# Cross-attention block in fp32: bias copies placed ahead of the normalised rows, and three early steps placed anew

## The chip, the cores and the metric

The kernel runs on one core of a Trainium2 chip. The metric is device time in microseconds (us) of one execution; lower is better. Before the change the median of three runs is 1100.1 us (1099.98 to 1101.31).

A core has five engines that run side by side: TensorE (PE; its weight loads are shown apart as PEld), VectorE (DVE), ScalarE (ACT), GpSimd (POOL) and SyncE (SP). Here SyncE issues every transfer (DMA). Each engine works through its own instructions in the order of the program and waits on semaphores where it needs another's result.

## The reference

Sixteen batches, each of 1024 query rows and 64 context rows, width 512, 16 heads of width 32. Query rows and context rows are each normalised, scaled and shifted by a conditioning vector; then cross-attention, a projection and a residual:

```
xq  = (1 + scale_q)  * layernorm(x)       + bias_q      # scale, bias from silu(cond) @ Wss_q
xkv = (1 + scale_kv) * layernorm(context) + bias_kv
q = xq @ Wq + bq ;  k, v = xkv @ Wkv + bkv
out = x + (softmax(q k^T / sqrt(32)) v) @ Wp + bp
```

All is fp32; x is (16, 1024, 512).

## The kernel before

**Tiles and stages.** The 16384 query rows are cut into 32 blocks of 512 (`NB = 32`; two blocks a batch, four tiles of 128 rows a block). Keys and values are made for two batches at a time, since 2 x 64 context rows fill the 128 partitions. A block i passes through these steps, each a small function in the code:

- `load_x` (L127) fetches its rows; `q_stats` (L260, VectorE) takes mean and variance; `q_scale` makes the factors (ScalarE, VectorE, GpSimd); `hidden` (L281, ScalarE) writes the normalised rows, two tiles a call.
- `turn` (L409, VectorE) and `move` (L421, SyncE) transpose them: 32x32 transposes into the one `ht` buffer, then 16 transfers of 64 KB into `xt`.
- `queries(i, o)` (L452): four matmuls of 128x512 into a PSUM bank, copied out to `qt` by ScalarE (L479). `query_weights` folds the scale into Wq first.
- `scores(i, z)` (L483): 32 small matmuls for one half of the keys; VectorE takes maxima (L501), then ScalarE copies the scores to SBUF (L508).
- `maxima`, `subtract` (spread on VectorE, L522, then GpSimd, L535), `weights` (L541, the exponential on ScalarE), `sums` (L546, VectorE), `inverse` and `divide` (L566, GpSimd).
- `mix(i)` (L570): 64 small matmuls, weights times values, copied out to `ot` by ScalarE.
- the projection. Blocks 0 and 1, and the last ones, use `project` (L610), four matmuls of 128x512 for each row tile. The loop, for blocks 2 to 28, uses seven products of half-size blocks instead of eight (`product`, L696), with three sums of half rows on VectorE (`row_sums`, L680), one on GpSimd (`last_row_sum`), and sums of the halves of Wp made once by `weight_sums` (L638, four subtractions on GpSimd into `WT`, and `b_diff`).

**Order of work.** It is written out by hand, under a manual schedule: the functions are called in the order in which each engine is to issue. A prologue handles blocks 0 to 2, a loop handles i = 3 to 29, and an end part the last two. In a turn i of the loop, the scores of block i, the queries of block i+1, mix and products of block i-1 and normalisation of block i+2 are interleaved.

**The projection's bias.** For i > 3 the loop calls `biased(i - 1)` (L661): two ScalarE copies (L665), which put the second half of the bias and the difference of its halves into PSUM banks 2 and 3; products 1 and 2 then accumulate onto them. In turn 3 there is no such call; products 1 and 2 start their banks themselves, and GpSimd adds the bias to the residual rows (`residual`, L286). Later blocks get the rest by one GpSimd add (`residual_rest`, L655). `added` (L724, VectorE) adds a bank to the residual rows. Query banks come from banks 0 and 1 in the loop (`ring`).

**The queue.** SyncE issues all transfers in program order. Eight completion semaphores are used in turn, so a transfer is issued only when the one eight places before it has landed. The Wp load (`load_projection`, L176) stands between the bias load and `move(1)`.

The calls in the loop around which the change is made:

```python
        hidden(i + 2, (0, 1))      # L897
        mix(i - 1)
        mixed_halves(i - 1)        # L677, L678
        hidden(i + 2, (2, 3))
        if i > 3:
            biased(i - 1)          # L902
        ...
        queries(i + 1, 1)          # L914
        product(i - 1, 1, first=i == 3)
        product(i - 1, 2, first=i == 3)
```

Of the kernel before, what the change touches and what calls it, by code (L numbers as in the profile page):

```python
# [20 lines left out]
def cross_attention_block(  # L21
# [101 lines left out]
    def rows_of(a, i):  # L123
        b, s = divmod(i, BPB)
        return a[b, s * TB : (s + 1) * TB, :].rearrange("(t p) h -> p t h", p=P)

    def load_x(i):  # L127
        t = xpool.tile([P, NT, H], F32, tag="x", name=f"x_{i}")
        nc.sync.dma_start(t, rows_of(x, i))
        x_tiles[i] = t  # L130

    def load_residual(i):

        tag = "r" if i < NB - 1 else "x"
        r = xpool.tile([P, NT, H], F32, tag=tag, name=f"r_{i}")
        nc.sync.dma_start(r, rows_of(x, i))
        r_tiles[i] = r
# [38 lines left out]
    def load_projection():  # L176
        nc.sync.dma_start(w_p_sb, w_p.rearrange("(c p) o -> p c o", p=P))
# [66 lines left out]
    def row_stats(mv, r):  # L244
        bs = small.tile([P, 6], F32, tag="bs", name="bs")
        nc.vector.bn_stats(bs, r)  # L246
        nc.vector.bn_aggr(mv, bs)

    def rstd_of(mv, n, tag):

        rstd = small.tile([P, 2, n], F32, tag=f"rstd{tag}", name=f"rstd{tag}")
        nc.scalar.activation(rstd[:, 0, :], mv[:, :, 1], AF.Sqrt, bias=eps_sb)
        nc.vector.reciprocal(rstd[:, 0, :], rstd[:, 0, :])
        nc.gpsimd.tensor_tensor(rstd[:, 1, :], mv[:, :, 0], rstd[:, 0, :], ALU.mult)
        nc.gpsimd.tensor_scalar(rstd[:, 1, :], rstd[:, 1, :], -1.0, None, ALU.mult)  # L255
        return rstd
# [3 lines left out]
    def q_stats(i, ts=range(NT)):  # L260
        if ts[0] == 0:
            q_mv[i] = small.tile([P, NT, 2], F32, tag="mvq", name=f"mvq_{i}")
        for t in ts:
            row_stats(q_mv[i][:, t, :], x_tiles[i][:, t, :])

    def q_scale(i):
        q_rstd[i] = rstd_of(q_mv.pop(i), NT, "q")
# [13 lines left out]
    def hidden(i, ts):  # L281

        for t in ts:
            normalise(x_tiles[i][:, t, :], x_tiles[i][:, t, :], q_rstd[i], t)

    def residual(i, ts=range(NT)):  # L286
        for t in ts:
            nc.gpsimd.tensor_add(r_tiles[i][:, t, :], r_tiles[i][:, t, :], b_p_sb)
# [9 lines left out]
    def context_features(b):  # L298
        hk = hk_tiles.pop(b)
        pt = bank(f"pkt_{b}")  # L300
        for c in range(NC):
            nc.tensor.transpose(pt[:, c * P : (c + 1) * P], hk[:, c * P : (c + 1) * P], ident)
        xk = kvpool.tile([P, NC, P], F32, tag="xk", name=f"xk_{b}")
        sk = ss["kv"]
        for c in range(NC):
            for j in range(2):
                at = c * P + j * LKV
                nc.scalar.activation(
                    xk[:, c, j * LKV : (j + 1) * LKV],
                    pt[:, at : at + LKV],  # L310
                    AF.Identity,
                    scale=sk[:, c, b + j : b + j + 1],
                    bias=sk[:, NC + c, b + j : b + j + 1],
                )
        xk_tiles[b] = xk
# [105 lines left out]
    def move(i):  # L421

        ht = ht_tiles.pop(i)
        xt = qpool.tile([P, 4, NC, NT * 32], F32, tag="xt", name=f"xt_{i}")
        for k in range(4):
            for g in range(4):
                nc.sync.dma_start(  # L427
                    xt[32 * k : 32 * k + 32, g],
                    ht[32 * g : 32 * g + 32, k].rearrange("p c t b -> p c (t b)"),
                )  # L430
        xt_tiles[i] = xt
# [20 lines left out]
    def queries(i, o, spare=False, later=False):  # L452

        xt, b = xt_tiles[i], i // BPB
        if o == 0:
            qt_tiles[i] = qpool.tile([P, NC, TB], F32, tag="qt", name=f"qt_{i}")
        if spare:
            pq = ps_s.tile([P, 2, TB], F32, tag="s", name=f"pq_{i}_{o}")[:, 0, :]
        else:
            pq = bank(f"pq_{i}_{o}")  # L460
        for c in range(NC):
            nc.tensor.matmul(  # L462
                pq.rearrange("p (g n) -> p g n", g=4),
                lhsT=wq_tiles[b][:, c, o * P : (o + 1) * P],
                rhs=xt[:, :, c, :],
                start=(c == 0),
                stop=(c == NC - 1),
            )
        pq_tiles[i, o] = pq
        if not later:  # L470
            queried(i, o)
# [61 lines left out]
    def subtract(i, eng=nc.gpsimd, zs=(0, 1)):  # L533
        for z in zs:
            eng.tensor_tensor(s_tiles[i, z], s_tiles[i, z], mb_tiles[i], ALU.subtract)  # L535
# [3 lines left out]
    def weights(i, z):  # L539
        p = s_tiles[i, z]  # L540
        nc.scalar.activation(p, p, AF.Exp, scale=SCALE)  # L541
# [96 lines left out]
    def weight_sums():  # L638
        t1, t2, t3, t4 = (WT[:, j] for j in range(4))
        nc.gpsimd.tensor_tensor(t1, half_weights(0, 1), half_weights(0, 0), ALU.subtract)  # L640
        nc.gpsimd.tensor_tensor(t2, half_weights(1, 1), t1, ALU.subtract)
        nc.gpsimd.tensor_tensor(t3, half_weights(1, 1), half_weights(0, 1), ALU.subtract)
        nc.gpsimd.tensor_tensor(t4, half_weights(1, 0), t2, ALU.subtract)
        nc.gpsimd.tensor_tensor(b_diff, b_first, b_second, ALU.subtract)
# [16 lines left out]
    def biased(i):  # L661

        for k, n, b in ((2, 1, b_second), (3, 2, b_diff)):
            acc[k] = bank(f"pp_{i}_{n}", k)
            nc.scalar.copy(acc[k].rearrange("p (t h) -> p t h", t=2), twice(b))  # L665
# [96 lines left out]
    load_x(2)  # L762
    load_residual(0)
    load_projection_bias()
    load_projection()
    for h in range(2):
        scale_shift_rows("kv", h)
    turn(1, range(NT))
    move(1)
    load_x(3)  # L770
    queries(0, 2)
    for h in range(2):
# [13 lines left out]
    load_x(4)  # L786
    load_residual(1)
    residual(0)
    weight_sums()
    value_products(0)  # L790
    scores(0, 1)
    maxima(0)
# [50 lines left out]
    scores(2, 1)  # L843
    maxima(2)
    subtract(2)
    hidden(4, (2, 3))
    project(0, 3)
    queries(3, 0)
# [5 lines left out]
    mix(1)  # L854
    mixed(1)
    q_stats(5)
    queries(3, 3)
    weights(2, 0)
    project(1, 0)
    sums(2, 0)  # L860
    weights(2, 1)
    residual(2, (0, 1))
    project(1, 1)
    sums(2, 1)
    inverse(2)
    divide(2)
    q_scale(5)
    context_features(2)
    query_weights(2)
    project(1, 2)  # L870
# [2 lines left out]
    for i in range(3, NB - 2):  # L873
        nxt3 = i + 3 < NB
        kvb = i // 4 * 2 + 2
        kv = i % 4 if kvb < B else None
        if nxt3:
            load_x(i + 3)
        if kv == 0:
            load_context(kvb)  # L880
        if i > 3:
            added(i - 2, 5)
        scores(i, 0)
        if i > 3:
            product(i - 2, 4)
            added(i - 2, 4)
            product(i - 2, 3)
            added(i - 2, 3)
        else:
            project(i - 2, 3)  # L890
            ring[:] = [0, 1]
        scores(i, 1)
        maxima(i)
        subtract(i)
        queries(i + 1, 0)
        load_residual(i)
        hidden(i + 2, (0, 1))  # L897
        mix(i - 1)
        mixed_halves(i - 1)
        hidden(i + 2, (2, 3))  # L900
        if i > 3:
            biased(i - 1)  # L902
        if kv == 1:
            context_hidden(kvb)
        if nxt3:
            q_stats(i + 3)
        if kv == 0:
            kv_stats(kvb)
        row_sums(i - 1)
        turn(i + 2, range(NT))  # L910
        move(i + 2)
        if not nxt3:
            load_residual(NB - 1)
# [3 lines that stand above are left out]
        weights(i, 0)  # L917
        added(i - 1, 1)
        added(i - 1, 2)
        sums(i, 0)  # L920
        weights(i, 1)
        queries(i + 1, 2)
        last_row_sum(i - 1)
        if i == 3:
            residual(2, (2, 3))
        if i < NB - 3:
            residual_rest(i)
        else:
            residual(i)
        product(i - 1, 6)  # L930
        product(i - 1, 7)
        sums(i, 1)
        added(i - 1, 6)
        inverse(i)
        added(i - 1, 7)
        divide(i)
        if nxt3:
            q_scale(i + 3)
        if kv == 0:
            kv_scale(kvb)  # L940
        if kv == 2:
            context_features(kvb)
        if kv == 3:
            keys(kvb)
        queries(i + 1, 3)
        if (i + 2) % BPB == 0 and i + 2 < NB:
            query_weights((i + 2) // BPB)
        if kv == 3:
            value_products(kvb)
            value_tiles(kvb)  # L950
        product(i - 1, 5)
# [95 lines left out]
```

## Time and profile before

| what | value |
|---|---|
| median of three runs | 1100.1 us |
| the profiled execution's own time | 1099.69 us |
| its span, first to last instruction | 1097.9 us |
| TensorE busy | 1079.0 us (98%) |
| VectorE busy | 874.1 us (80%) |
| ScalarE, GpSimd busy | 656.7, 661.0 us (60% each) |
| bias copies (L665), one | 587 to 590 ns, 52 of them |
| DMA moved | 145.36 MB |

The profile comes from one execution. Times in its rows count from the start of the span. In a row of the groups or the timeline, the name before the arrow is written and those behind it are read; "x16" counts instructions. "Idle before" is the time that the engine stood still ahead of the row, with what ended it; a chain lists the work that ended last, followed back from the end. A weight load (PEld) may run under the matmul before it, and then costs nothing.

### The profile page before, as it was taken

What the parts mean: (1) busy time and instruction counts of PE and PEld (TensorE: products, weight loads), DVE (VectorE), ACT (ScalarE), POOL (GpSimd) and SP (SyncE); (2) the same over time, 40 slices, a digit from 0 to 9 for tenths busy, and PEclk for the clock granted to TensorE, in tenths of its full rate; (3) what the DMA queues carried; (4) which work ended last, traced back from release to release, by engine and by line L of the source; (5) the groups of instructions that cost most, each with busy time, mean ns of one, the idle gap of its engine ahead of it and who ended that gap; (6) DMA issues with size and microseconds to landing.
All of it is one profiled execution on the core that took longest, in us unless ns stands there. A gap on an engine that the chain in (4) does not pass through costs nothing.

```text
span 1097.9 us, 20355 instructions
## 1 busy us (share of the span) xinstructions
PE 1079.0 (98%) x8290; PEld 612.1 (56%) x8290; DVE 874.1 (80%) x1132; ACT 656.7 (60%) x804; POOL 661.0 (60%) x288
## 2 busy tenths in 40 slices
PE   6999999999999999999999999999999999999998
PEld 4534365555655557555565556555665556655533
DVE  4699678888698886989868889688887888697893
ACT  3576656657467573766736676465765657467430
POOL 0447685666747765666737666566765666748830
PEclk9999999999999999999999999999999999999999
DMA  9633432444234443344443343343342444333302
GB/s 354 218 113 116 152 122 98 143 151 153 89 110 144 141 144 112 115 135 140 137 143 125 116 142 123 130 154 119 129 144 92 144 154 136 96 109 104 134 29 87
DMA packets 80524, 145.36 MB, mean 132 GB/s; under 512 B 10504, under 2 KB 10656, under 8 KB 80432
## 3 DMA queue, kind: packets, MB, share of 16 engines
q1 hardware_dynamic: 80432, 144.07, 39.3%
q8 instruction: 65, 1.06, 0.4%
q14 instruction: 27, 0.22, 0.1%
HBM read 77.97 MB, written 33.55 MB: 102 GB/s over the span
## 4 chain that ended last, share of the span: by engine, by line
PE 92%; DMA 3%; DVE 2%; ACT 1%; SPq 1%; issue 0%; DVEq 0%
PE pq L462 38%; PE pp L715 31%; PE po L586 7%; PE ps L490 6%; PE pp L613 6%; PE pv L350 2%; PE pk L322 2%; DMA w_kv_sb<-in_L_xcond_Wkv_dram 1%; DMA w_p_sb<-in_L_xcond_Wp_dram 1%; DVE m L501 1%; SPq L144 1%; DMA x<-in_x_dram 1%; SPq L427 1%; DVE vb L522 0%; DVE l L546 0%; ACT s L541 0%
## 5 line engine op out<-in xcount | busy, mean ns | idle before, releaser
L462 PE MATMUL pq<-xt,wq 128*128 128x512 f32 x1024 | 465.9, 599 | 1.8 <-DMA xt<-ht 1.7
L566 POOL TENSOR_TENSOR s<-s,vb 128x2048 f32<-128x2048 f32 x62 | 279.9, 4536 | 192.8 <-DVE vb L522 183.4
L535 POOL TENSOR_TENSOR s<-s,mb 128x2048 f32<-128x2048 f32 x58 | 262.6, 4553 | 160.9 <-DVE mb L522 158.8
L462 PEld LDWEIGHTS pq<-xt,wq 128*128 128x128 f32 x1024 | 188.4, 190 | 244.0 <-issue 240.4
L508 ACT COPY s<-ps 128x1024 f32<-128x1024 f32 x128 | 129.6, 1012 | 196.2 <-DVE m L501 188.7
L729 DVE TENSOR_TENSOR r<-pp,r 128x512 f32<-128x512 f32 x189 | 126.4, 669 | 72.4 <-PE pp L715 71.5
L479 ACT ACTIVATE qt<-pq,bqs 128x512 f32<-128x512 f32 x128 | 87.7, 686 | 154.2 <-PE pq L462 153.4
L501 DVE TRANSPOSE_TENSOR_REDUCE m<-ps 128x32 f32<-128x1024 f32 x128 | 152.2, 1227 | 24.3 <-PE ps L490 24.3
L715 PE MATMUL pp<-w_p_sb,ot 128*128 128x256 f32 x648 | 151.4, 384 | 0.0
L546 DVE TRANSPOSE_TENSOR_REDUCE l<-s 128x64 f32<-128x2048 f32 x64 | 146.2, 2299 | 5.7 <-ACT s L541 5.2
L715 PEld LDWEIGHTS pp<-w_p_sb,ot 128*128 128x128 f32 x648 | 121.2, 190 | 35.5 <-ACT pp L665 19.9
L541 ACT ACTIVATE s<-s 128x2048 f32<-128x2048 f32 x64 | 121.9, 1910 | 21.0 <-POOL s L535 16.3
L715 PE MATMUL pp<-WT,ot 128*128 128x256 f32 x432 | 104.9, 386 | 0.0
L715 PE MATMUL pp<-WT,s 128*128 128x256 f32 x432 | 102.8, 381 | 0.0
L715 PEld LDWEIGHTS pp<-WT,s 128*128 128x128 f32 x432 | 81.6, 190 | 32.1 <-issue 19.8
L277 ACT ACTIVATE x<-x,rstdq 128x512 f32<-128x512 f32 x128 | 96.9, 810 | 1.9 <-POOL rstdq L255 1.9
L715 PEld LDWEIGHTS pp<-WT,ot 128*128 128x128 f32 x432 | 80.0, 190 | 32.3 <-DVE r L729 16.8
L246 DVE BATCH_NORM_STATS2 bs<-x 128x6 f32<-128x512 f32 x128 | 84.4, 659 | 2.2 <-DMA x<-in_x_dram 2.2
L414 DVE STREAM_TRANSPOSE ht<-x 128x512 f32<-128x512 f32 x124 | 77.5, 679 | 5.9 <-DMA xt<-ht 3.8
L522 DVE STREAM_TRANSPOSE mb<-m 128x2048 f32<-128x2048 f32 x32 | 74.0, 2312 | 6.1 <-POOL s L566 2.7
L490 PE MATMUL ps<-qt,kt 32*32 32x512 f32 x2048 | 76.6, 600 | 1.8 <-DVE kt L330 0.8
L586 PE MATMUL po<-s,vt 32*32 32x512 f32 x2048 | 76.1, 599 | 1.2 <-ACT qt L479 1.2
(94 smaller groups left out, 904.5 us busy)
## 6 DMA issues: line engine op xcount, KB each, us to landing
x<-in_x_dram SPq DMA_DIRECT2D x32, 1024.0 KB, 5.7
r<-in_x_dram SPq DMA_DIRECT2D x32, 1024.0 KB, 5.4
xt<-ht SPq DMA_DIRECT2D x496, 64.0 KB, 2.0
out_dram<-r SPq DMA_DIRECT2D x54, 512.0 KB, 2.8
out_dram<-r SPq DMA_DIRECT2D x20, 256.0 KB, 2.0
wss_q<-in_L_xcond_Wss_q_dram SPq DMA_DIRECT2D x2, 1024.0 KB, 9.0
ctx<-in_ctx_dram SPq DMA_DIRECT2D x8, 256.0 KB, 5.6
wss_kv<-in_L_xcond_Wss_kv_dram SPq DMA_DIRECT2D x2, 1024.0 KB
```

The source lines that it names most:

```text
L277: nc.scalar.activation(dst, src, AF.Identity, bias=rstd[:, 1, j : j + 1], scale=rstd[:, 0, j : j + 1])
L462: nc.tensor.matmul(pq.rearrange("p (g n) -> p g n", g=4), lhsT=wq_tiles[b][:, c, o * P : (o + 1) * P], rhs=xt[:, :, c, :], start=(c == 0), ...
L490: nc.tensor.matmul(pss[r // 2][32 * c : 32 * c + 32, r % 2, :], lhsT=kt[rows, c, z * HK : (z + 1) * HK], rhs=qt[rows, c, :], start=True, s ...
L501: nc.vector.tensor_reduce(m_tiles[i][:, z, 2 * e : 2 * e + 2, :], pss[e].rearrange("p r (j a) -> p r j a", a=32), AX.X, ALU.max, apply_tra ...
L508: nc.scalar.copy(s_sb[:, 2 * e : 2 * e + 2, :], pss[e])
L535: eng.tensor_tensor(s_tiles[i, z], s_tiles[i, z], mb_tiles[i], ALU.subtract)
L541: nc.scalar.activation(p, p, AF.Exp, scale=SCALE)
L546: nc.vector.tensor_reduce(l_tiles[i][:, z], s_tiles[i, z].rearrange("p r (j a) -> p r j a", a=32), AX.X, ALU.add, apply_transpose=True,)
L566: eng.tensor_tensor(s_tiles[i, z], s_tiles[i, z], vb, ALU.mult)
L586: nc.tensor.matmul(po[c][32 * r : 32 * r + 32, :], lhsT=vt[rows, z, 32 * r : 32 * r + 32], rhs=p[rows, r, :], start=(z == 0), stop=(z == 1),)
L715: nc.tensor.matmul(acc[k][:, t * HO : (t + 1) * HO], lhsT=rows[:, c, t * P : (t + 1) * P], rhs=cols[:, c, :], start=new and t == 0 and c == 0,
L729: nc.vector.tensor_add(r, acc[k].rearrange("p (t h) -> p t h", t=2), r)
```

## The change

Five calls of the hand-written order are placed elsewhere. No operation is added, removed or altered.

1. In the loop, `biased(i - 1)` is called ahead of `hidden(i + 2, (0, 1))`, `mix` and `mixed_halves`, no longer behind the second `hidden`.
2. `load_projection()`, the 1 MB load of Wp, is called behind `move(1)` and ahead of `load_x(3)`.
3. `weight_sums()`, which reads Wp, goes from behind `residual(0)` to behind `subtract(2)`.
4. `weights(2, 0)`, an exponential of block 2, is called ahead of `queries(3, 3)`. On TensorE this changes nothing; on ScalarE the exponential now stands before the copy of that query bank.
5. `residual(2, (0, 1))`, GpSimd's bias add for half of block 2, goes behind `divide(2)` and `q_scale(5)`.

```diff
@@ prologue
     load_projection_bias()
-    load_projection()
     for h in range(2):
         scale_shift_rows("kv", h)
     turn(1, range(NT))
     move(1)
+    load_projection()
     load_x(3)
@@
     residual(0)
-    weight_sums()
     value_products(0)
@@
     scores(2, 1)
     maxima(2)
     subtract(2)
+    weight_sums()
     hidden(4, (2, 3))
@@
     q_stats(5)
+    weights(2, 0)
     queries(3, 3)
-    weights(2, 0)
     project(1, 0)
     sums(2, 0)
     weights(2, 1)
-    residual(2, (0, 1))
     project(1, 1)
     sums(2, 1)
     inverse(2)
     divide(2)
     q_scale(5)
+    residual(2, (0, 1))
     context_features(2)
@@ loop
         load_residual(i)
+        if i > 3:
+            biased(i - 1)
         hidden(i + 2, (0, 1))
         mix(i - 1)
         mixed_halves(i - 1)
         hidden(i + 2, (2, 3))
-        if i > 3:
-            biased(i - 1)
         if kv == 1:
             context_hidden(kvb)
```

## The prediction, made before the changed kernel ran

> **What bounds the kernel now.** I read the page first: busy shares, then the chain that ended last.
>
> ```profile
> span 1097.9 us, 20355 instructions
> ...
> PE 1079.0 (98%) x8290; PEld 612.1 (56%) x8290; DVE 874.1 (80%) x1132; ACT 656.7 (60%) x804; POOL 661.0 (60%) x288
> ...
> PE 92%; DMA 3%; DVE 2%; ACT 1%; SPq 1%; issue 0%; DVEq 0%
> ```
>
> TensorE is busy nearly throughout and carries 92% of the chain. So time can come only from TensorE's few waits (early) and from matmul groups that run slower than they need. The list of all waits names both.
>
> ```profile
> PEld pp L715 <- ACT pp L665: 19.9, 26, 0.8
> ...
> DVE ht L414 <- DMA xt<-ht: 3.8, 1, 3.8
> ...
> PE pq L462 <- DMA xt<-ht: 1.7, 1, 1.7
> ```
>
> Columns: total us, times, longest. The first row is the bias copy holding the weight loader, 26 times for 0.77 us. Only part of this is lost, because the loader works under running matmuls. What is lost is seen in the chain in order of time (start, us), where turn 3 of the loop makes the same products without bias copies (145.47) and turn 4 with them (183.71):
>
> ```profile
> 141.84 3.63 PE pq L462 x8
> 145.47 3.45 PE pp L715 x16
> ...
> 180.08 3.63 PE pq L462 x8
> 183.71 3.66 PE pp L715 x16
> 187.37 3.43 PE pq L462 x8
> 190.80 3.45 PE pp L715 x16
> ```
>
> The group costs 3.66 with the copies and 3.45 without. The timeline of that place shows why:
>
> ```profile
> 181.10 0.59 ACT L678 COPY ot<-po 128x512 f32<-128x512 f32 x1
> ...
> 181.58 1.52 ACT L277 ACTIVATE x<-x,rstdq 128x512 f32<-128x512 f32 x2
> ...
> 183.00 0.59 ACT L665 COPY pp<-b_p_sb 128x512 f32<-128x512 f32 x1
> ...
> 183.65 3.32 PEld L715 LDWEIGHTS pp<-w_p_sb,ot 128*128 128x128 f32 x16 [0.77 <-ACT pp L665]
> ```
>
> The first copy ends at 183.59; the load starts at 183.65, when the previous group is already over, instead of 0.43 us after the load at 182.69 (183.12). The load (0.19) is then exposed.
>
> The early place is a transfer. SyncE's timeline, and its own waits:
>
> ```profile
> 29.83 0.37 SPq L177 DMA_DIRECT2D w_p_sb<-in_L_xcond_Wp_dram  x1
> 31.78 14.47 SPq L427 DMA_DIRECT2D xt<-ht  x16
> ...
> SPq L427 <- DMA w_p_sb<-in_L_xcond_Wp_dram: 3.5, 1, 3.5
> ```
>
> The 16 moves of block 1 take 14.47 us to issue, against 10.36 for the moves at 84.40. The eighth waits for w_p's landing (39.72) because it reuses that load's completion semaphore; the first four land only at 39.98 to 40.48, right behind w_p.
>
> **What the Trainium skill says.** "TensorE: Matmul & The Clock Gate" (Architectural detail) says that TensorE's queue can pull a weight load ahead of matmuls in flight, while ScalarE is strictly first in, first out. The trace agrees: 3.43 to 3.45 where the load was early, about 0.2 more where it was not; and L665 runs in its place in ScalarE's order though its banks were free long before. "DMA: Bandwidth & Descriptors" (Queues, rings and completion order) says that each DMA engine takes descriptors in ring order. The moves that land right behind w_p agree. The same page (Anatomy of one DMA) says that waits are made by the issuing sequencer; 36.17 to 39.74 on SyncE is one.
>
> **Part 1: bias copies ahead of the normalised rows** (turns 4 to 29). No work is added. In turn 4: the ACT copy of pq ends near 178.5; the two copies then take about 1.03 (183.00 to 184.03), the two normalisations 1.5, so L677 starts near 180.9 (before 180.20, where it had waited 0.27 for PE) and L678 ends near 182.4 (before 181.69). Banks: their last readers, the VectorE adds, start by 173.14, so end by 173.83. The first product now waits for L678 at 182.4; the load wants to go at 183.12: 0.7 to spare. Gain 0.21 x 26 = 5.5 us. Bounds: 0 to 0.21 each, since no run shows these turns with the copies earlier; I take the whole, because turn 3 shows it.
> What is behind on ACT: the first half of the normalised rows 1.03 later, L677/L678 0.7 later, the second half 0.7 later; the next qt copy waits for PE (183.7) anyway. Who waits: VectorE's sums read the L677/L678 rows. In turn 5 VectorE gets there at 213.5 (four statistics at 0.8 from 210.31), L678 ends near 213.4, L685 needs only L677 (213.0): nothing. Its transposes come three sums (1.8 us) later, behind both halves. In turn 29, without statistics, the sums slip 0.7 once, with 7 us before their product. Cost nothing; with that cover gone, at most 0.7 us of VectorE a turn.
>
> **Part 2: w_p behind block 1's moves.** w_p held the DMA engines from b_p's landing (35.63) to 39.72. Without it the eighth move issues at 36.2 and the sixteenth 8 x 0.635 later, at 41.3; 2.0 to 2.4 us later it has landed: 43.5. TensorE is ready at 46.45 (end of scores at 45.30 + 1.15): the whole 1.65 goes. VectorE's transposes of block 2 start at 44.15 instead of 47.98. Following both on:
> - VectorE's first maxima end at 49 (before 52.7), so ScalarE's score copies end at 50.0, no longer delaying the qt copies; its last qt copy of block 1 ends at 61.4 (63.56). The scores at 62.21, which waited for it, finish 2.2 earlier rather than 1.65.
> - VectorE: exponentials end at 60.0, sums 62.35, spread 65.6, maxima, statistics, then m of the second half at 72.2 (74.86). This releases the qt copy for which mix waited 1.19 at 78.90: now 76.25, 2.6 earlier.
> - The scores at 96.17 run 1.60 rather than 1.15 for the same sort of reason; 0.2 of that goes. Sum 2.8 us, kept: TensorE has no wait from 97.7 to 133, and the wait there (0.66 at 133.71) follows VectorE's work that starts from TensorE's own product at 121.1.
> Its price: w_p (1024 KB) and x_3 are issued at about 42, land by about 51 (5.7 alone, plus 4.1 for the one ahead), in front of block 2's moves, issued from 46.7. Two of those reuse these semaphores, as seventh and eighth, at 50.5 and 51.1: covered. xt lands near 59; wanted at 62.5. w_p's first reader is the projection near 82. Bounds for this part: 0 (all absorbed) to 3.8 (what VectorE gains).
>
> **Part 3: the weight sums** (four of 1.28 and one of 0.73, 5.8 us of GpSimd) go from 41.86 to behind the subtraction that ends at 119.14. GpSimd then is idle 9.32 to 130.97, plus 2.50 of the moved bias add: covered with 6 us over. Their first reader is at 152. **Part 4: the bias add of block 2** (2 of 1.25) now stands behind the division (140.4): the next subtraction starts at 142.95 instead of 142.47, so its second exponential is 0.5 later, its block's division 0.5 later (ends 169.2), which mix wants at 177.73. Nothing. **Part 5: the exponential ahead of a qt copy**: it may run 1.8 to 2.5 us earlier, but VectorE's sums behind it wait for the projection's product (8.38 before 121.15); the qt copy is 1.4 later, its bank wanted four banks on, at 124.75. Nothing. Bounds for 3 to 5 together: -0.3 to +0.5.
>
> Sum: 1097.9 - 5.5 - 2.8 = 1089.6 span; the profiled execution lay 1.8 above its span (1099.69), so 1091.4; the runs' median (1100.1) is 0.4 above it: 1091.8.
>
> **Rivals.**
> - *The early gain is absorbed*: block 2's moves are slowed behind w_p and x_3, and TensorE waits at 62.5 for them. For it: they share the engines from 46.7. Against: 3.5 us to spare. It decides once xt lands after 65. -5.5: 1094.6.
> - *The load is not early again*: another wait takes its place, L678, now 0.7 later. Against: 0.7 to spare by the durations above. Only part 2 stays: 1097.3.
> - *Slower*: ScalarE's order. If the copies in their new place cost more than 1.03 (a bank not free, or a copy slowed beside running matmuls), L677 and L678 move with them, and with them the first product in 26 turns. It decides at L678 ending 1.2 us later than worked out (183.6: no gain); at 1.5 later it loses 0.3 x 26 = 7.8, less 2.8: 1105.1. Against it: the banks free 4 us before.
> - *No change*: both gains only shift the wait, 1100.
>
> **How the numbers follow.** Forecast 1091.8: 0.72. Early gain absorbed 0.12; load not early 0.07; no change 0.04; slower 0.05. A change within 0.2% (2.2 us) can't be told from none here. The 1097.3 case just passes it, so faster 0.90, same 0.05, slower 0.05. The forecast's own range is 1090.5 to 1093.4 (1100.1 - 5.5, less 1.7 to 3.8 for part 2, and the 0.3 and 0.5 of parts 3 to 5); to hold 8 in 10 the range takes in the absorbed case, up to 1095.0.
>
> **What would show it.** Right: the bias copy gone from the loader's waits; products 1 and 2 in 3.45 in every turn; a turn in which TensorE makes no keys or values in 30.83 instead of 31.04 (174.17 to 205.21); the queries at 48.10 starting near 46.45, the transposes at 47.98 near 44.15, the projection at 84.5 near 81.9. Wrong: the loader waiting for L678 (part 1), a wait for xt near 62.5 (part 2), a wait of mix for GpSimd near 139 (part 3), of VectorE's L685 for ACT (part 1's cover).

## The result, and the profile after

The changed kernel takes 1092.51 us in the median (four runs, 1090.73 to 1093.65) against 1100.7 us (four runs): a ratio of 0.9924, 95% interval 0.9907 to 0.9941. The forecast was 1091.8, with a range of 1090.0 to 1095.0. The profiled execution has a span of 1090.0 us, against 1097.9 before and 1089.6 forecast.

From the page of the changed kernel, the span, the busy times and the chain by engine:

```profile
span 1090.0 us, 20329 instructions
...
PE 1073.0 (98%) x8290; PEld 612.9 (56%) x8290; DVE 874.7 (80%) x1132; ACT 655.7 (60%) x804; POOL 661.5 (61%) x288
...
PE 92%; DMA 3%; DVE 2%; ACT 1%; SPq 1%; issue 0%; DVEq 0%
```

The shares are the same as before: the kernel is still bound by TensorE, and no other engine has taken its place. TensorE's busy time fell by 6.0 us although it runs the same matmuls; in part that is because the first matmul behind an exposed load is recorded as longer (up to 484 ns in the products before, against 379 in the median).

The list of waits of the changed kernel (total us, times, longest):

```profile
DVE s L685 <- ACT ot L678: 3.0, 1, 3.0
...
DVE ht L414 <- DMA xt<-ht: 2.1, 1, 2.1
```

The row of the bias copy (19.9 us, 26 times) is gone, and so is TensorE's wait for xt. The VectorE wait for L678 occurs once, as before (2.4 then, 3.0 now): that is turn 29, where the cover of the statistics is missing. VectorE's wait for the moves fell from 3.8 to 2.1, not to nothing.

The chain of the changed kernel in order of time (start, us), turns 3 and 4:

```profile
139.27 3.63 PE pq L462 x8
142.90 3.45 PE pp L715 x16
...
177.50 3.63 PE pq L462 x8
181.14 3.45 PE pp L715 x16
```

Turn 4 now makes its first two products in 3.45, as turn 3 always did (3.66 before). The timeline of ScalarE and of the weight loader at that place:

```profile
175.85 0.59 ACT L665 COPY pp<-b_p_sb 128x512 f32<-128x512 f32 x1
...
179.19 0.58 ACT L678 COPY ot<-po 128x512 f32<-128x512 f32 x1
179.67 1.53 ACT L277 ACTIVATE x<-x,rstdq 128x512 f32<-128x512 f32 x2
...
180.54 0.19 PEld L715 LDWEIGHTS pp<-w_p_sb,ot 128*128 128x128 f32 x1 [0.24 <-ACT x L277]
```

L678, the last thing that the first product needs of ScalarE, ends at 179.77. The weight load starts at 180.54, 0.42 us after the one before it at 180.12, so it runs under the queries. There are 0.77 us to spare. From the start of these queries to the start of the next ones, the 26 turns take 6.99 us each, against 7.20 before.

The early place, on SyncE's timeline and TensorE's:

```profile
30.90 10.91 SPq L427 DMA_DIRECT2D xt<-ht  x16
41.86 0.58 SPq L177 DMA_DIRECT2D w_p_sb<-in_L_xcond_Wp_dram  x1
...
45.51 14.20 PE L462 MATMUL pq<-xt,wq 128*128 128x512 f32 x32
```

The 16 moves are issued in 10.91 us instead of 14.47. TensorE begins block 1's queries at 45.51 instead of 48.10, with no wait. VectorE's transposes of block 2, which wait for the last move, and TensorE's first projection move by the same amount. The two lines of the kernel before, then those of the changed one:

```profile
47.98 2.49 DVE L414 STREAM_TRANSPOSE ht<-x 128x512 f32<-128x512 f32 x4 [3.83 <-DMA xt<-ht]
84.51 7.03 PE L613 MATMUL pp<-w_p_sb,ot 128*128 128x512 f32 x16
...
45.40 2.49 DVE L414 STREAM_TRANSPOSE ht<-x 128x512 f32<-128x512 f32 x4 [2.12 <-DMA xt<-ht]
81.94 7.03 PE L613 MATMUL pp<-w_p_sb,ot 128*128 128x512 f32 x16
```

The projection follows 36.53 us behind the transposes before and 36.54 after. The last projection work of the run starts 7.90 us earlier than before (1085.62 against 1093.52); 2.57 of this are there when the first projection starts (81.94 against 84.51), and 26 x 0.206 = 5.4 come from the turns.

### The profile page after: what moved, and what is told of

The parts are those of the page before. It is cut to its first block, busy times and chain, and to the rows that moved or that the text cites. A ratio compares the mean times of both kernels' runs of the same rounds, so it can differ in the third digit from the quotient of the medians.

```text
span 1090.0 us, 20329 instructions
## 1 busy us (share of the span) xinstructions
PE 1073.0 (98%) x8290; PEld 612.9 (56%) x8290; DVE 874.7 (80%) x1132; ACT 655.7 (60%) x804; POOL 661.5 (61%) x288
## 4 chain that ended last, share of the span: by engine, by line
PE 92%; DMA 3%; DVE 2%; ACT 1%; SPq 1%; issue 0%; DVEq 0%
PE pq L462 38%; PE pp L715 31%; PE po L586 7%; PE ps L490 6%; PE pp L613 6%; PE pv L350 2%; PE pk L322 2%; DMA wss_kv<-in_L_xcond_Wss_kv_dram 1%; DMA b_p_sb<-in_L_xcond_bp_dram 1%; DVE m L501 1%; DMA x<-in_x_dram 0%; SPq L427 0%; DVE vb L522 0%; DVE l L546 0%; DMA xt<-ht 0%; ACT s L541 0%
## 5 line engine op out<-in xcount | busy, mean ns | idle before, releaser
L715 PE MATMUL pp<-w_p_sb,ot 128*128 128x256 f32 x648 | 148.7, 379 | 0.0
```

What stands on the lines that cost most here:

```text
L715: nc.tensor.matmul(acc[k][:, t * HO : (t + 1) * HO], lhsT=rows[:, c, t * P : (t + 1) * P], rhs=cols[:, c, :], start=new and t == 0 and c == 0,
```

## The experiments

Each ratio is to the kernel before, run beside it on the same chip: one chip for the first four runs, a second for the next four, a third for the last three. A saving in us is worked out from the ratio.

**The bias copies alone.**

```diff
+        if i > 3:
+            biased(i - 1)
         hidden(i + 2, (0, 1))
         ...
         hidden(i + 2, (2, 3))
-        if i > 3:
-            biased(i - 1)
```

> The kernel before with the bias copies alone placed ahead of the normalised rows (part 1). My theory: products 1 and 2 of turns 4 to 29 take 3.45 us instead of 3.66, the bias copy vanishes from the weight loader's waits, the span falls by 26 x 0.21 = 5.5 us to about 1092.4; queries of block 1 still start near 48.1. Rival (the loader's wait is not the copies', or another takes its place): the group stays at 3.66 and the time at 1100.

Measured: ratio 0.9951 (0.9939 to 0.9964), 5.4 us less. Products 1 and 2 take 3.45 in every turn, and block 1's queries start at 48.07. By the two medians (1095.57 and 1100.33) it is 4.8. This part of the gain, and its cause, stand.

**w_p alone.**

```diff
     load_projection_bias()
-    load_projection()
     ...
     move(1)
+    load_projection()
     load_x(3)
```

> The kernel before with the w_p load alone behind block 1's moves; the weight sums stay where they were, ahead on GpSimd, and must now wait for w_p. My theory: the last move of block 1 lands about 2.6 us earlier, VectorE's transposes of block 2 start near 45.4 instead of 47.98, the projection at 84.5 starts near 81.9, span about 1095.3; the sums end by about 57, before GpSimd's first division near 66, so that leaving them costs nothing. Rival 1 (part of the early gain in the changed kernel was the first 18 us, which ran 0.87 us faster before w_p was ever issued): only 1.7 is left, span about 1096.2. Rival 2 (the early gain is absorbed without the moved sums): span 1097.9.

Measured: ratio 0.9981 (0.9974 to 0.9987), 2.1 us less (1.4 to 2.9). That lies between the theory (2.6) and rival 1 (1.7) and decides neither. The transposes of block 2 start at 45.22. But leaving the sums in place is not free. GpSimd's timeline of this run, then VectorE's:

```profile
51.89 1.28 POOL L642 TENSOR_TENSOR WT<-w_p_sb 128x512 f32<-128x512 f32 x1
53.13 3.32 POOL L643 TENSOR_TENSOR WT<-w_p_sb,WT 128x512 f32<-128x512 f32 x1
56.41 2.78 POOL L644 TENSOR_TENSOR b_diff<-b_p_sb 128x256 f32<-128x256 f32 x1
```

```profile
52.74 2.58 DVE L535 TENSOR_TENSOR s<-s,mb 128x2048 f32<-128x2048 f32 x1
55.24 0.74 DVE L363 TENSOR_TENSOR vt<-pv,b_v_sb 128x256 f32<-128x256 f32 x2
55.91 2.69 DVE L535 TENSOR_TENSOR s<-s,mb 128x2048 f32<-128x2048 f32 x1
```

The sums wait for w_p until 49.31 and then run beside VectorE's two subtractions. Two of the sums take 2.05 us longer than the 1.27 and 0.73 of the kernel before; the subtractions take 2.58 and 2.69 instead of 2.29 and 2.28 (the kernel before and the changed one). That is 0.7 us on the very chain of VectorE that w_p's move speeds up; VectorE's sums behind them take 0.2 less (4.49, not 4.69). What arrives at TensorE is 0.45: mix goes on 31.37 us after the transposes' start, against 30.92 in the kernel before and in the changed one. The projection starts at 83.86 and not near 81.9, because the queries before it (78.67) also take 5.36 instead of 3.70, in a stretch at half the TensorE clock (see the last section). The Trainium skill, "GPSIMD Engine Reference" (Specifications), says that GpSimd shares its SBUF interfaces with VectorE and that they contend when VectorE's instruction has two SBUF inputs; these subtractions have two, and the trace agrees.

**The three small ones alone**: the weight sums, the exponential and the bias add of block 2.

```diff
     residual(0)
-    weight_sums()
     ...
     subtract(2)
+    weight_sums()
     ...
+    weights(2, 0)
     queries(3, 3)
-    weights(2, 0)
     ...
-    residual(2, (0, 1))
     ...
     q_scale(5)
+    residual(2, (0, 1))
```

> The kernel before with only the weight sums, the exponential of block 2 and the bias add of block 2 placed anew (parts 3 to 5). My theory: no difference, span 1097.9 within 0.5 us, since VectorE's sums of block 2 start behind the projection's product at 121.2 wherever the exponential stands. Rival (the earlier exponential lets the sums of block 2 start earlier): the wait of the scores at 133.7 shrinks, span down by up to 1.7.

Measured: ratio 1.0003 (0.9994 to 1.0011), no difference. The scores' wait is still 0.66.

**ScalarE's order, the other way.** The changed kernel, with both halves of the normalised rows ahead of L677 and L678.

```diff
         mix(i - 1)
-        mixed_halves(i - 1)
         hidden(i + 2, (2, 3))
+        mixed_halves(i - 1)
```

> The changed kernel with both halves of the normalised rows ahead of the copies L677 and L678 (in turns 3 to 29), so that L678 ends 1.5 us later. In the changed kernel L678 ends at 179.77 in turn 4 and the first product's weight load starts at 180.54: 0.77 to spare. My theory (the load needs only that its last ScalarE work ends 0.6 us ahead of the queries' end): L678 now ends at 181.3, the load starts there, the pair of products takes about 0.4 us longer in 27 turns, span about 1090.0 + 11 = 1101, and the loader waits for ACT L678. Rival (any order of ScalarE's work before the product gives the early load as long as the bias copies stand first): 1090.

Measured: 1103.33 us, ratio 1.0024 (1.0015 to 1.0032): slower than the kernel before, and 11 us behind the changed one, though the bias copies still stand first. The weight loader's waits and its timeline in turn 4:

```profile
PEld pp L715 <- ACT ot L678: 24.6, 27, 0.9
```

```profile
181.29 0.19 PEld L462 LDWEIGHTS pq<-xt,wq 128*128 128x128 f32 x1 [0.24 <-issue]
182.41 3.32 PEld L715 LDWEIGHTS pp<-w_p_sb,ot 128*128 128x128 f32 x16 [0.94 <-ACT ot L678]
```

L678 ends at 182.37, the load starts at 182.41. From queries to queries, 26 turns take 7.37 instead of 6.99 (turn 3 stays at 6.99): 9.7 us of the 11.8 between the two profiles. Another 1.15 is there before the first projection (83.09 against 81.94), in an execution with a slower start (first queries at 18.92 against 18.11). The last 0.9 is lost in the end part, where the scores at 1053.06 take 2.05 instead of 1.14; why was not followed up.

So what counts is not the copies as such, but when ScalarE's last work for the load ends. The queries of these turns last 3.54 us when nothing holds the group behind them. In turn 3 of this run L678 ends 0.53 us ahead of their end, the load follows 0.10 us later, and nothing is lost. In the kernel before, the first bias copy ends 0.05 us behind their end, and a turn loses 0.21. Here L678 ends 0.22 behind, and a turn loses 0.37: 0.17 later costs 0.17 more. No run lies between 0.53 ahead and 0.05 behind. The slower rival of the prediction was a real one, and the 0.77 us to spare decided against it.

**The other loads behind block 2's moves as well.**

```diff
     move(1)
-    load_projection()
-    load_x(3)
     ...
     move(2)
+    load_x(3)
+    load_projection()
```

> The changed kernel with the loads of x_3 and w_p behind block 2's moves as well. In the changed kernel the last move of block 1, issued at 41.23 with these two loads right behind it in the queue, landed 3.75 us later (44.98) instead of 2.0, and VectorE began block 2's transposes at 45.40. My theory (the two loads slow the moves just ahead of them): the last move lands near 43.3, the transposes start at 44 or earlier, right behind VectorE's maxima, 1.2 us sooner; TensorE, ready for block 1's queries at about 45.5 anyway, gains up to 1 us at the copies it waits for near 61 and 76; span about 1089. x_3 lands near 62, wanted at 68. Rival (the last move takes 3.75 for another reason): no difference, 1090.0.

Measured: ratio 0.9926 (0.9913 to 0.9938); the changed kernel beside it, below, has 0.9922. No difference, the rival holds. The transposes start at 44.36, but the same loads behind block 2's moves together with the next edit give 45.88, and eight executions with the loads in the changed kernel's place, or with w_p alone there, lie between 44.13 and 46.55 (mean 45.25). The last move lands 2.71 us after its issue here and 2.02 with the next edit added, against 2.02 to 4.00 in those eight. The spread of 2.4 us is one between executions. In most of them one or two issues of a move take 1 to 2 us instead of 0.59 (1.27 here); neither that nor the late landing is explained.

**The sums of block 2 first.** In the changed kernel VectorE still waits 8.37 us for the projection's product at 118.57, with the sums queued behind.

```diff
     queries(3, 3)
+    sums(2, 0)
     project(1, 0)
-    sums(2, 0)
     weights(2, 1)
-    project(1, 1)
     sums(2, 1)
     inverse(2)
     divide(2)
+    project(1, 1)
```

> The changed kernel with VectorE's sums of block 2 called ahead of the projection products that they stood behind (sums(2, 0) ahead of project(1, 0); sums(2, 1), inverse and divide ahead of project(1, 1)). My theory: the earlier exponential, which gains nothing by itself, now lets VectorE use 2 to 3 us of its 8.4 us wait near 118; its maxima of block 3 start before TensorE's scores need them, the scores' wait at 131.14 (0.66, and 1.07 more inside them) goes: 1.7 us less, span about 1088.3. Rival (another wait takes its place, as GpSimd's division or a bank that the delayed projection add frees late): 1090.

Measured: 1090.01 us, ratio 0.9904 (0.989 to 0.9917). TensorE's timeline of this run:

```profile
124.44 1.14 PE L490 MATMUL ps<-qt,kt 32*32 32x512 f32 x32
125.51 3.70 PE L613 MATMUL pp<-w_p_sb,ot 128*128 128x512 f32 x8
129.14 1.14 PE L490 MATMUL ps<-qt,kt 32*32 32x512 f32 x32
```

and the changed kernel's:

```profile
125.70 1.14 PE L490 MATMUL ps<-qt,kt 32*32 32x512 f32 x32
126.77 3.70 PE L613 MATMUL pp<-w_p_sb,ot 128*128 128x512 f32 x8
131.14 2.22 PE L490 MATMUL ps<-qt,kt 32*32 32x512 f32 x32 [0.66 <-ACT s L508]
```

The second scores wait no more: they end 5.84 us after the first ones began, not 7.66. These 1.8 us are close to the 1.9 by which the medians differ (1091.9 and 1090.01).

**Both of these edits together.**

> The two edits of the runs on the loads behind block 2's moves and on the sums of block 2, together. They act at different places (44 to 78 and 116 to 133), so their gains add: span about 1087.5, median about 1090. Rival: one takes away the cover of the other, no better than the better of the two alone.

Measured: 1090.38 us, ratio 0.9905 (0.9889 to 0.992): the sums' gain and nothing of the loads'.

**The changed kernel again**, beside these three.

> The changed kernel itself once more, beside the three variants on the same chip: ratio 0.992 to 0.993 to the kernel before, span near 1090.

Measured: 1091.9 us, ratio 0.9922 (0.9908 to 0.9935).

**All but the bias copies**: the changed kernel with `biased(i - 1)` back behind the second `hidden`.

> The changed kernel with the bias copies back behind the second half of the normalised rows: parts 2 to 5 without part 1. It closes the sum. My theory: the parts are independent, so this is the kernel with w_p alone moved: ratio 0.998, about 2.2 us below the kernel before, products 1 and 2 back at the slower length in 26 turns. Rival (the moved sums or the exponential add to w_p's gain): ratio 0.997, 3 us or more.

Measured: 1096.93 us, ratio 0.9962 (0.9949 to 0.9976), 4.2 us less (2.6 to 5.6), more than w_p alone (2.1); the rival is the nearer. In its trace the sums no longer meet VectorE's subtractions, which take 2.29 and 2.28, and the projection starts at 81.13. Of the 2.1 between the two runs the contention accounts for about 0.45. Another part may be the clock: 9 of the 19 executions of w_p alone have a mean clock of 0.998 (median 1099.1; the other ten 1098.05), and none of the five here. The rest was not separated; the two intervals touch. The sum closes to about 1 us: 5.4 for the bias copies and 4.2 here make 9.6, and the whole change is 8.4 (6.5 to 10.2).

**The sums first, but the exponential at its old place.** The edit is against the version with the sums first.

```diff
-    weights(2, 0)
     queries(3, 3)
+    weights(2, 0)
     sums(2, 0)
```

> The kernel with VectorE's sums of block 2 first, but with the exponential back behind the queries (part 5 undone). My theory: part 5 is what makes the earlier sums possible. With the exponential at its old place it ends about 2.4 us later, VectorE's sums start near 117.7 instead of 115.3, the maxima of block 3 are late again and the scores wait as in the changed kernel: span near 1090 (or 1.5 to 2 more than with the exponential first). Rival (the sums' place alone does it): span near 1088.

Measured: 1092.23 us, ratio 0.9919 (0.9905 to 0.9932), as the changed kernel. VectorE then waits 8.89 us for the exponential, and the scores wait 0.46 and run 2.22. So the exponential's new place gains nothing in the changed kernel, but it is what the earlier sums need.

**The sums first, again**, beside the two above.

> The kernel with VectorE's sums of block 2 first once more, beside the two above on one chip: ratio to the kernel before 0.990 to 0.991, without the scores' wait near 131.

Measured: 1090.01 us, ratio 0.9903 (0.9889 to 0.9917), the same as the first time. This version has the lowest median of all that ran.

## Why the prediction was right

**Part 1, the bias copies: right in place, cause and size.** Forecast 5.5 us; 26 x 0.206 = 5.4 in the trace, and 5.4 (4.0 to 6.7) with this part alone. ScalarE's new order went as worked out: 0.7 to spare was forecast, 0.77 measured. The bound from 0 to 0.21 a turn was rightly taken at its upper end, because turn 3 in the old profile was a ready-made comparison. Behind ScalarE only the sums of turn 29 slipped, by 0.6 (0.7 was forecast); in turn 5 the sums L685 start at 210.70, straight behind the statistics.

**Part 2, w_p: right in place and cause, near in size partly by luck.** Forecast 2.8 us; the difference at the first projection is 2.57.
- What decides is when block 1's last move has landed. VectorE's transposes of block 2 wait for it, and in the kernel before and in seven other profiles the first projection starts 36.53 to 36.54 us after them. The remaining five profiles have the contention or a half-clock stretch in between.
- The last move was to issue at 41.3 and issued at 41.23, but it was to land 2.0 to 2.4 us later and landed 3.75 later (44.98). So the transposes began at 45.40, 2.58 earlier than before and not 3.83 (44.15), and these 2.58 are the gain.
- The prediction let only 2.6 of its 3.83 through to mix. TensorE was to begin the queries at 46.45, 2.3 us behind the transposes, and ScalarE, which copies them out, was to end its exponentials at 60.0. That case did not occur: in all thirteen profiles the queries begin within 0.14 us of the transposes. In the first run with the sums first these start as early as forecast, the queries at 44.18; the exponentials end at 59.13, and the full 3.85 arrives at the projection:

```profile
44.13 2.49 DVE L414 STREAM_TRANSPOSE ht<-x 128x512 f32<-128x512 f32 x4 [2.43 <-DMA xt<-ht]
80.66 7.03 PE L613 MATMUL pp<-w_p_sb,ot 128*128 128x512 f32 x16
```

- The 0.2 forecast for the scores at 96.17 did not come: they still run 1.59 (at 93.60).

So 2.6 and 2.57 agree, but in the forecast TensorE's queries held the gain down, and in the trace the late landing did. That they came out alike is luck. TensorE was ready at 45.51, not 46.45, since its first 18 us ran 0.87 faster (first queries at 18.11 against 18.98), before w_p is issued in either kernel. That is a difference between executions; no run shows whether the gain would have been smaller without it. The size also varies from one execution to the next: with w_p behind, the transposes start between 44.13 and 46.55 (mean 45.25), with it ahead at 47.95, 47.98 and 49.30. By the ratio this part, with those after it, is worth 4.2 (2.6 to 5.6), by the two medians 3.8; the forecast lies inside the interval.

**Part 3, the weight sums: priced at nothing, for their new place rightly.** Division 2 is not delayed and they end at 122.36. What the prediction did not see is that in the old place, behind a later w_p, they would have run into VectorE's subtractions. Moving them spares part 2 about 0.45 us; without w_p's move, parts 3 to 5 together change nothing (1.0003).

**Parts 4 and 5: nothing, as forecast.** The reason given for the exponential, that VectorE's sums stand behind the projection's product, is shown by the runs with the sums first: they gain with the exponential ahead and not with it behind.

**The rivals.** The early gain was not absorbed: xt of block 2 landed by about 60.1 and was wanted at 62.1, with 2 us to spare rather than 3.5. The load was early again. The slower rival needed L678 1.2 us later; with it 1.4 later by design (3.76 after the queries begin, against 2.34) the kernel was slower than before by 0.24% (0.15 to 0.32).

## What to carry to other kernels

Look for matmul groups of one kind that differ by about a weight load in length: the longer ones may wait for something just before they start, even where the list shows TensorE itself without a wait. Ask the weight loader's waits which. Not every such difference is a wait that can be moved: here the pair of products behind scores takes 3.65 in all 27 turns, before and after. What has to end early is the last work that the load waits for, so order the other engine's queue by the deadline of each result, and count how much is to spare before moving anything ahead of it. A bulk load that nobody needs soon belongs behind the small transfers on the path, and what reads it has to be moved along, away from an engine that it would contend with.

## What the runs showed of the hardware

- In six of the thirteen profiles the clock record has a stretch of 3.41 or 6.83 us at half the TensorE clock in the early part. Each begins within a wait of TensorE or up to 2.7 us behind its end: at 47.4 and 50.5 with the bias copies alone and with the three small ones (waits of 3.61 and 2.62 us for xt), near 78 with w_p alone and in two runs with the sums first (waits of 1.2 for mix), at 132.8 with the loads behind block 2's moves (a wait of 0.66 for the scores). The queries of block 1 take 14.18 in the profile before and 17.04 in the one with the bias copies alone. Windows of TensorE in that run (us, busy and matmuls, clock, DMA share, GB/s):

```profile
48.00:54.90 6.90, 6.83 (x9) 0.55 0.57 194
54.90:66.00 11.10, 11.10 (x43) 1.00 0.52 152
```

  Nine matmuls in the first stretch, at a mean clock of 0.55; the kernel before has 16 in 48.00 to 55.00. Other profiles have none after waits of 1.2 for mix and of up to 1.65 for xt (the kernel before). The two longest waits, 3.61 and 2.62, both have one. Whether the wait is the cause was not tested.
- Where GpSimd's and VectorE's subtractions met, the one that began second stood still for nearly as long as the first still had to run. GpSimd's two began with 2.19 us of VectorE's left and took 2.05 longer; VectorE's two began with 0.43 and 0.54 of GpSimd's left and took 0.29 and 0.41 longer. So each engine lost by turns, and in all four meetings 0.13 or 0.14 less than what was left of the other. They were seen in one execution.
- One issue of a 64 KB transfer in a row of 16 often takes 1.0 to 2 us where the others take 0.59, with and without a large load behind it. The last transfer of the row landed 2.0 to 4.0 us after its own issue. The two do not go together: with the longest slow issue (1.91) it landed after 2.02.
